# Near positions of keys in two half arrays, and the own block's part added before the write, in a disentangled attention

## The chip, the cores and the metric

The kernel runs on one core of a Trainium2 chip. The metric is the time on the device in microseconds, from the start to the end of one execution. The kernel before took 2058.43 us, the median of three runs (2057.97 to 2059.12).

## The reference, cut to what matters

The program is a chain of four layers on 8 x 512 tokens of 256 channels: an attention with relative positions, a feed-forward layer, a second attention and a layer of routed experts. The change lies in the first attention alone.

```python
q, k, v = split_heads(x @ Wq + bq), split_heads(x @ Wk + bk), split_heads(x @ Wv + bv)   # 16 heads of 16
scores = einsum('bhqd,bhkd->bhqk', q, k) / scale
rel = build_relative_position(S, S, 64, 128)            # buckets of q - k
pos_k = (rel_embeddings @ Wk + bk) by head              # 128 positions
c2p = take_along_axis(einsum('bhqd,hpd->bhqp', q, pos_k), clip(rel + 64, 0, 127))
p2c = take_along_axis(einsum('bhkd,hpd->bhkp', k, pos_k), clip(-rel + 64, 0, 127)) transposed
out = softmax(scores + (c2p + p2c) / scale) @ v
```

The score of a query and a key has three parts: their product; `c2p`, a product of the query with a position that depends on the distance; and `p2c`, a product of the key with such a position. The last one is found by key and has to be turned, so that it lies by query.

## The kernel before, in words

The first attention is cut into 256 steps: 8 batch elements (b), 4 groups of four heads (g), 4 blocks of 128 rows (i), 2 pairs of heads (p). The list `steps` has them in this order, so that a step and the step two later have neighbouring blocks of the same pair of heads. The order of all instructions is written out by hand (`manual_schedule`); each engine takes its own in that order, and waits at semaphores.

For step u, `strips(u)` (it is called in the iteration of step u - 5, `AHEAD`) multiplies 128 queries and 128 keys of two heads with a table of 256 distances. That gives four strips of 128 x 256 (tile `strip`, index 2 j + t: head j; t = 0 by query, t = 1 by key). ScalarE copies them out of PSUM (L371). A row's entry for column c lies at a distance from the diagonal, so the rows have to be shifted against one another. This is done through DRAM: SP writes the strips into a scratch tensor `shift` of rows of 512 (L381), and reads it back with a row step of 511 (L390), which moves each row by one column. In what is read, `winc` has query rows and the key columns of three blocks (two at the first and last block), `winp` has key rows and query columns likewise: 128 x 2 heads x 384 or 256 columns. There are four scratch tensors.

Distances beyond the table have all the value of its last column, `strip[..., W - 1]`. In the own block (key block equal to query block) one triangle lacks it. GpSimd multiplies that value with two triangular masks (`own` from `aside`, L374) and adds the result to the middle block of `winp` and of `winc` (L401), once they are read.

The order on SP's queue is: the write of strip u, then the two reads of strip u - 1 (the list `reads` holds one back). On GpSimd: `own` of u, then the adds of u - 2 (the list `adds` holds two back), then whatever the plan puts into the step.

An iteration n of the main loop does, in the order in which TensorE gets it: products of queries and keys into the score banks `sc` (L421) interleaved with the strips of n + 5 (L364); `near_keys` for each of two heads, which turns the blocks of `winp` and adds them to `sc` (L433: 128 x 128, by a matmul with the identity in transpose mode); VectorE then adds `winc` and finds the row's lowest value (`e`, L447), ScalarE takes the exponential (L450); the turning of the exponentials of the step before (L461, 64 x 64 pieces in alternating halves of the array), which VectorE copies out (L464); and products with the values (L473). `near_keys(n)` reads the windows of steps n - 2, n and n + 2: of n + 2 the first of three blocks, which `own` does not touch. At the last block (i = 3) nothing of n + 2 is needed.

The table `plan` puts further work into certain steps: projections of the next group (L174, two more matmuls of 512 columns twice a step), turning of inputs, values, and the end of a batch element (`finish`), whose `norm` puts six GpSimd operations into each of two successive steps (L521 to L523).

Of the kernel before, what the change touches and what calls it, by code (L numbers as in the profile page):

```python
# [12 lines left out]
F32 = mybir.dt.float32  # L13
# [3 lines left out]
ALU = mybir.AluOpType  # L17
# [4 lines left out]
P = 128  # L22
B, S, H = 8, 512, 256
NT = S // P
# [4 lines left out]
W = 256  # L29
WIN = 3 * P  # L30
# [60 lines left out]
def _l0_attention(nc, tc, a, x, ident, mhalf, carry, prefetch):  # L91
# [6 lines left out]
    with ExitStack() as ctx:  # L98
        pool = lambda name, bufs, **kw: ctx.enter_context(tc.tile_pool(name=name, bufs=bufs, **kw))
        wp = pool("a_w", 1)  # L100
# [44 lines left out]


        winc, cleared = [None] * (2 * NT), list(vs)
        for p in range(2):
            for i, width in ((0, S + 2 * P), (1, S + 3 * P)):
                w = wp.tile([P, 2, width], F32, tag=f"winc{i}{p}", name="winc")  # L150
                cleared.append(w)
                winc[2 * i + p], winc[2 * (NT - 1 - i) + p] = w[:, :, :S], w[:, :, width - S :]
# [37 lines left out]
        with tc.tile_pool(name="a_pos", bufs=1) as pp:  # L190
# [87 lines left out]
            with tc.manual_schedule():  # L278
                nc.vector.memset(pk, 0.0)
                for w in cleared[:3]:  # L280
                    nc.vector.memset(w, 0.0)
                busy(3, zeros)
                measure[0]()
                for n, c in enumerate((P - 1, 0)):
                    f = pp.tile([P, NH, HD], F32, tag=f"end{n}", name=f"end{n}")
                    position_keys(lambda k: relT[:, k, c : c + 1].to_broadcast([P, P]), f)
                    ends.append(f)
                position_keys(lambda k: relT[:, k, :], pk[:, :, :HD])
                some = products()
                next(some)  # L290
                norm[0]()
                next(some)
                measure[1]()
                next(some)
                norm[1]()
                for g in range(NG):
                    for t, dst in ((0, posc), (1, posp)):
                        pe = ps_a.tile([P, S], F32, tag="psa", name="pe")
                        nc.tensor.matmul(
                            pe[:, :W], pk[:, 4 * g : 4 * g + 4, :].rearrange("p h e -> p (h e)"), oh[:, t, :], start=True, stop=True  # L300
                        )
# [24 lines left out]
                for w in cleared[3:]:  # L326
                    nc.vector.memset(w, 0.0)

        sb = pool("a_sb", 2)
# [12 lines left out]
        reads, adds = [], []  # L342
        cns = {b: [] for b in range(B)}
        rest = []
        def project(b, g):
# [10 lines left out]
        def strips(u, between=None):  # L356


            b, g, i, p = steps[u]
            s = sm[b, g]  # L360
            pas = [ps_a.tile([P, S], F32, tag="psa", name="pa") for j in range(2)]
            for t, (src, pos) in enumerate(((s[0], posc), (s[2], posp))):
                for pa, rs in zip(pas, heads(p)):
                    nc.tensor.matmul(  # L364
                        pa[:, t * W : (t + 1) * W], src[rs, i * P : (i + 1) * P], pos[rs, g, :], start=True, stop=True
                    )
                if t == 0 and between is not None:
                    between()
            st = sb.tile([P, 4, W], F32, tag="strip", name="strip", bufs=3)
            for j in range(2):  # L370
                nc.scalar.copy(st[:, 2 * j : 2 * j + 2, :].rearrange("p t w -> p (t w)"), pas[j])  # L371

            own = sb.tile([P, 2, 2, P], F32, tag="own", name="own", bufs=3)
            nc.gpsimd.tensor_tensor(  # L374
                own,
                aside.unsqueeze(2).to_broadcast([P, 2, 2, P]),
                st[:, :, W - 1 : W].rearrange("p (j t) o -> p t j o", t=2).to_broadcast([P, 2, 2, P]),
                ALU.mult,
            )
            d = shift[u % NSHIFT]  # L380
            nc.sync.dma_start(  # L381
                bass.AP(d.tensor, d.offset + P + 1, [[2 * W, P], [2 * W * P, 4], [1, W - 1]]), st[:, :, : W - 1]
            )
# [14 lines left out]

            def add():
                for t, dst in ((1, wk_[:, :, P : 2 * P]), (0, wc[:, :, i * P : (i + 1) * P])):  # L400
                    nc.gpsimd.tensor_tensor(dst, dst, own[:, t], ALU.add)  # L401


            reads.append(read)
            adds.append(add)
# [23 lines left out]
        def near_keys(n, j, sc):  # L429
            i = steps[n][2]  # L430
            lo, hi, c0, c1 = near(i)
            for m in range(lo, hi):
                nc.tensor.matmul(  # L433
                    sc[:, m * P : (m + 1) * P],
                    wins[n + 2 * (m - i)][1][:, j, (i - m + 1) * P : (i - m + 2) * P],
                    ident,
                    start=False,
                    stop=m == hi - 1,
                    is_transpose=True,
                    skip_group_check=True,  # L440
                )

        def weights(n, j, sc):
            b, g, i, p = steps[n]
# [90 lines left out]
        for b in range(B):  # L535
            n = 8 * NG * b
# [18 lines left out]
        with tc.manual_schedule():  # L555
# [9 lines left out]
            for now in range(len(steps) + 3):  # L565
                n = now
                if n < len(steps):
                    b, g, i, p = steps[n]
                    if (i, p) == (0, 0):
                        if g % 2 == 0:  # L570
                            totals[b, g // 2] = sb.tile([P, NT, 8], F32, tag="totals", name="totals", bufs=2)
                    scs, parts = products(n)
                    parts.pop(0)()
                    more = parts.pop() if parts else None
                    if n + AHEAD < len(steps):
                        strips(n + AHEAD, more)
                    else:
                        if more is not None:
                            more()
                        for todo in (reads, adds):  # L580
                            if todo:
                                todo.pop(0)()
                    new = []
# [1087 lines left out]
def _constants():  # L1671
# [12 lines left out]
    for k in range(NK):  # L1684
# [4 lines left out]
    return {  # L1689
        "onehot": onehot,  # L1690
        "tail": tail,
        "later": np.tril(np.ones((P, P), np.float32), -1),
        "before": before,
        "heads": heads,
        "pages": (P * (m[:, None] + P * np.arange(2))).astype(np.float32),
# [74 lines left out]
```

## Time and profile before

| What | Value |
|---|---|
| median of three runs | 2058.43 us |
| profiled execution, its own time | 2059.9 us |
| span from first to last instruction of that execution | 2058.1 us |
| granted TensorE clock, mean of the span | 0.978 |
| first attention, from the first to the last turning of near positions | 44.3 to 1062.3 us |
| TensorE busy in 44 to 1062 us | 993.3 us |
| DMA share and rate in 44 to 1062 us | 0.95, 300 GB/s |
| GpSimd busy in 44 to 1062 us | 732.7 us |
| DMA share in 1062 to 2058 us | 0.43 |

A row of the page's fifth part names line, engine and operation, the output and inputs by the program's names, and the count; then the busy time in us and the mean duration of one in ns; then the idle time of the engine just before such instructions, and what ended most of it. "SPq" is the queue of SP, which issues DMAs; the number behind a kind of DMA is the median time from issue to landing. TensorE's busy time is modelled where matmuls overlap[...].

### The profile page before, as it was taken

How to read it: one execution, taken by the hardware profiler on the slowest of the kernel's cores; microseconds unless marked ns; L12 is line 12 of the kernel's file. 1: busy time of each engine (PE TensorE's matmuls, PEld its weight loads, DVE VectorE, ACT ScalarE, POOL GpSimd, SP SyncE). 2: the span in 40 equal slices, each digit the busy share in tenths (PEclk: the TensorE clock that was granted, in tenths of full speed). 3: DMA queues.
4: the chain of work that ended last, by engine and by line, in shares of the span. 5: the costliest groups of instructions: out<-in, count | busy, mean ns of one | idle time of the engine just before them, and what ended most of it. 6: DMA issues, size and time to landing. Idle time of an engine off the chain costs nothing. (4 is left out here: it accounts for less than half of the span.)

```text
span 2058.1 us, 49708 instructions
## 1 busy us (share of the span) xinstructions
PE 1946.7 (95%) x18056; PEld 1330.7 (65%) x18056; DVE 1393.1 (68%) x3727; ACT 1108.3 (54%) x2370; POOL 1133.2 (55%) x1334
## 2 busy tenths in 40 slices
PE   7999999999999999999989999989898887899997
PEld 4667667676666666666656666645555445588886
DVE  4767777777777777766776555257877786356766
ACT  3777777767776777777742221344343333144443
POOL 4666777867778676776833111014444443455555
PEclk9999999999999999999999999999999998899999
DMA  8999999999999999999964536801111115557888
GB/s 295 332 301 286 306 305 295 312 288 315 297 300 284 296 306 300 296 295 294 293 196 147 155 104 186 21 0 43 43 43 43 43 43 197 199 164 216 269 259 269
DMA packets 387522, 444.46 MB, mean 216 GB/s; under 512 B 43472, under 2 KB 368080, under 8 KB 386768
## 3 DMA queue, kind: packets, MB, share of 16 engines
q1 hardware_dynamic: 372496, 401.94, 64.0%
q0 software_dynamic: 13824, 38.29, 5.1%
q8 instruction: 146, 2.39, 0.5%
q10 hardware_dynamic: 960, 1.05, 0.2%
q14 instruction: 96, 0.79, 0.1%
HBM read 238.99 MB, written 202.19 MB: 214 GB/s over the span
## 5 line engine op out<-in xcount | busy, mean ns | idle before, releaser
L447 DVE CUSTOM_DVE_ANT_0 e<-sc,winc 128x512 f32<-128x512 f32 x512 | 333.4, 689 | 281.0 <-PE sc L433 157.8
L450 ACT ACTIVATE e<-e,low 128x512 f32<-128x512 f32 x512 | 365.6, 715 | 96.0 <-DVE low L447 94.9
L371 ACT COPY strip<-pa 128x512 f32<-128x512 f32 x512 | 275.0, 590 | 128.2 <-POOL winc L401 58.6
L374 POOL TENSOR_TENSOR own<-aside,strip 128x512 f32<-128x512 f32 x256 | 268.5, 1049 | 115.5 <-ACT strip L371 94.3
L464 DVE COPY et<-et_ps 128x512 f32<-128x512 f32 x512 | 328.7, 684 | 0.7 <-PE et_ps L461 0.7
L421 PE MATMUL sc<-sm,sm 32*128 32x256 f32 (+3 forms) x1792 | 309.2, 436 | 0.4
L364 PE MATMUL pa<-pos,sm 32*128 32x256 f32 x2048 | 291.7, 401 | 0.1
L941 POOL DMA_INDIRECT rows<-pay,slot x128 | 141.0, 1101 | 224.2 <-issue 210.9
L401 POOL TENSOR_TENSOR winp<-winp,own 128x256 f32<-128x256 f32 x256 | 186.9, 730 | 107.6 <-DMA winp<-shift 82.1
L421 PEld LDWEIGHTS sc<-sm,sm 32*128 32x128 f32 x1792 | 164.2, 184 | 96.9 <-DVE et L464 34.6
L433 PE MATMUL sc<-ident,winp 128*128 128x128 f32 x1280 | 203.8, 286 | 24.3 <-DMA winp<-shift 23.7
L941 POOL DMA_INDIRECT results<-y,r x160 | 156.0, 975 | 121.0 <-ACT y L1545 78.5
L401 POOL TENSOR_TENSOR winc<-winc,own 128x256 f32<-128x256 f32 x256 | 186.7, 729 | 58.4 <-DMA winc<-shift 48.2
L433 PEld LDWEIGHTS sc<-ident,winp 128*128 128x128 f32 x1280 | 137.1, 141 | 102.7 <-issue 57.9
L461 PE MATMUL et_ps<-ident,e 64*128 64x64 f32 x4096 | 184.1, 230 | 1.1 <-DVE et L464 1.1
L364 PEld LDWEIGHTS pa<-pos,sm 32*128 32x128 f32 x2048 | 175.9, 184 | 10.9 <-ACT strip L371 3.9
L58 POOL TENSOR_TENSOR rstd<-var,mhalf 128x2 f32<-128x2 f32 (+1 forms) x56 | 51.0, 911 | 235.2 <-DVE var L56 212.1
L461 PEld LDWEIGHTS et_ps<-ident,e 64*128 64x128 f32 x4096 | 148.8, 140 | 44.1 <-issue 21.5
L1525 PE MATMUL pge<-store,rT 128*128 x640 | 167.0, 384 | 2.3 <-DMA r<-rows 1.0
L473 PE MATMUL ctx_ps<-et,v 128*32 128x128 f32 x4096 | 167.4, 282 | 0.5 <-DVE et L464 0.5
L174 PE MATMUL pq<-xnT,wqk 128*128 128x512 f32 x256 | 133.3, 645 | 0.0
L738 ACT ACTIVATE hT<-ph,b 128x512 f32<-128x512 f32 x64 | 44.0, 687 | 165.7 <-PE ph L735 165.6
(222 smaller groups left out, 3357.5 us busy)
## 6 DMA issues: line engine op xcount, KB each, us to landing
shift<-strip SPq DMA_DIRECT2D x256, 510.0 KB, 4.5
winp<-shift SPq DMA_DIRECT2D x128, 384.0 KB, 5.4
winc<-shift SPq DMA_DIRECT2D x128, 384.0 KB, 5.5
winp<-shift SPq DMA_DIRECT2D x128, 256.0 KB, 4.1
winc<-shift SPq DMA_DIRECT2D x128, 256.0 KB, 4.4
rows<-empty SPq DMA_DIRECT2D x8, 2640.0 KB, 17.4
r<-rows SPq DMA_DIRECT2D x160, 132.0 KB, 2.5
z<-results SPq DMA_DIRECT2D x32, 512.0 KB, 5.1
```

Source lines behind the costliest of these rows:

```text
L364: nc.tensor.matmul(pa[:, t * W : (t + 1) * W], src[rs, i * P : (i + 1) * P], pos[rs, g, :], start=True, stop=True)
L371: nc.scalar.copy(st[:, 2 * j : 2 * j + 2, :].rearrange("p t w -> p (t w)"), pas[j])
L374: nc.gpsimd.tensor_tensor(own, aside.unsqueeze(2).to_broadcast([P, 2, 2, P]), st[:, :, W - 1 : W].rearrange("p (j t) o -> p t j o", t=2).t ...
L401: nc.gpsimd.tensor_tensor(dst, dst, own[:, t], ALU.add)
L421: nc.tensor.matmul(sc[:, c0:c1], s[side_][rs, cut : cut + P], s[2 + side_][rs, c0:c1], start=c0 == 0, stop=False, skip_group_check=True,)
L433: nc.tensor.matmul(sc[:, m * P : (m + 1) * P], wins[n + 2 * (m - i)][1][:, j, (i - m + 1) * P : (i - m + 2) * P], ident, start=False, stop ...
L447: nc.vector.tensor_tensor_reduce(e, sc, wins[n][0][:, j, :], 1.0, -LOW, ALU.add, ALU.min, low)
L450: nc.scalar.activation(e, e, AF.Exp, bias=low, scale=-1.0, accum_out=totals[b, g // 2][:, i, r : r + 1])
L461: nc.tensor.transpose(bank[:, c : c + 64], e[rs, m * P : (m + 1) * P], ident[rs, rs])
L464: nc.vector.tensor_copy(et[:, f].rearrange("p j m q -> p (j m q)"), bank)
L473: nc.tensor.matmul(ctx_ps[32 * r : 32 * r + 32, i * P : (i + 1) * P], vs[b % 2][:, m, g % 2, g // 2 * 4 + r, :], et[:, :, m, :], start=m = ...
L941: ins = nc.gpsimd.indirect_dma_start(to, bass.IndirectOffsetOnAxis(ap=index, axis=0), source, None, bounds_check=last)
```

## The change

The windows of `winp` get a new layout. Where before 128 rows held a block's keys and two heads side by side, now head j lies in rows 64 j to 64 j + 63, and the second index k is the half of the keys (64 each). For a middle block, the first half of the keys is read with columns 0 to 319 and the second with columns 64 to 383; what the other 64 columns would hold is zero, and is cleared once at the start. So a middle block's read has 320 columns in place of 384; an edge block's has 256 as before. A read of `winp` is now two DMAs, one for each head. The tiles are eight fixed ones in place of a rotating pool of eight.

`near_keys` turns pieces of 64 keys, for head 0 in the upper and head 1 in the lower half of the array, one after the other in turn: twice as many matmuls, each half as wide. It is called once for both heads, ahead of both heads' `e`.

The own block's part is added to the strips before they are written, in place of to the windows after they are read. `own` is the same product with other masks; one GpSimd addition of 128 x 2 x 2 x 128 elements puts it onto a half of each strip. The two additions to the windows, and the list `adds`, are gone. The write now follows the addition. `own` has two buffers in place of three, and the masks are loaded by one DMA.

```diff
+        winp = [wp.tile([P, 2, WIN], F32, tag=f"winp{n}", name=f"winp{n}") for n in range(2 * NT)]
...
-            nc.sync.dma_start(aside[:, 0, :], a["later"])
-            nc.sync.dma_start(aside[:, 1, :], a["earlier"])
+            nc.sync.dma_start(aside, a["aside"])
...
-                for w in cleared[3:]:
+                for w in cleared[3:] + [w.rearrange("p k c -> p (k c)")[:, WIN - 64 : WIN + 64] for w in winp]:
                     nc.vector.memset(w, 0.0)
...
-            own = sb.tile([P, 2, 2, P], F32, tag="own", name="own", bufs=3)
+            own = sb.tile([P, 2, 2, P], F32, tag="own", name="own", bufs=2)
             nc.gpsimd.tensor_tensor(
                 own,
-                aside.unsqueeze(2).to_broadcast([P, 2, 2, P]),
-                st[:, :, W - 1 : W].rearrange("p (j t) o -> p t j o", t=2).to_broadcast([P, 2, 2, P]),
+                aside.unsqueeze(1).to_broadcast([P, 2, 2, P]),
+                st[:, :, W - 1 : W].rearrange("p (j t) o -> p j t o", t=2).to_broadcast([P, 2, 2, P]),
                 ALU.mult,
             )
+            nearer = st.rearrange("p (j t) (h r) -> p j (t h) r", t=2, h=2)[:, :, 0:4:3, :]
+            nc.gpsimd.tensor_tensor(nearer, nearer, own, ALU.add)
             d = shift[u % NSHIFT]
             nc.sync.dma_start(
                 bass.AP(d.tensor, d.offset + P + 1, [[2 * W, P], [2 * W * P, 4], [1, W - 1]]), st[:, :, : W - 1]
             )
             wc = winc[u % (2 * NT)]
-            wk_ = sb.tile([P, 2, WIN], F32, tag="winp", name="winp", bufs=8)
+            wk_ = winp[u % (2 * NT)]

             def read():
                 lo, hi, c0, c1 = near(i)
-                for t, dst in ((1, wk_[:, :, c0:c1]), (0, wc[:, :, lo * P : hi * P])):
+                wide = c1 - c0 == WIN
+                step, c1 = 64 * (2 * W - 1) + 64 * wide, c1 - 64 * wide
+                for j in range(2):
+                    half = wk_[64 * j : 64 * j + 64]
+                    to = half[:, :, c0:c1]
+                    if wide:
+                        to = bass.AP(half.tensor, half.offset, [list(half.ap[0]), [WIN + 64, 2], [1, c1]])
                     nc.sync.dma_start(
-                        dst,
+                        to,
                         bass.AP(
                             d.tensor,
-                            d.offset + t * 2 * W * P + P + c0,
-                            [[2 * W - 1, P], [4 * W * P, 2], [1, c1 - c0]],
+                            d.offset + (4 * j + 2) * W * P + P + c0,
+                            [[2 * W - 1, 64], [step, 2], [1, c1 - c0]],
                         ),
                     )
-
-            def add():
-                for t, dst in ((1, wk_[:, :, P : 2 * P]), (0, wc[:, :, i * P : (i + 1) * P])):
-                    nc.gpsimd.tensor_tensor(dst, dst, own[:, t], ALU.add)
+                lo, hi, c0, c1 = near(i)
+                nc.sync.dma_start(
+                    wc[:, :, lo * P : hi * P],
+                    bass.AP(d.tensor, d.offset + P + c0, [[2 * W - 1, P], [4 * W * P, 2], [1, c1 - c0]]),
+                )
...
-            if len(adds) > 2:
-                adds.pop(0)()
...
+                for k in range(2):
+                    for j, sc in enumerate(scs):
+                        rs, c = slice(64 * j, 64 * j + 64), m * P + 64 * k
+                        nc.tensor.matmul(
+                            sc[:, c : c + 64],
+                            wins[n + 2 * (m - i)][1][rs, k, (i - m + 1) * P : (i - m + 2) * P],
+                            ident[rs, rs],
+                            start=False,
+                            stop=(m, k) == (hi - 1, 1),
...
-                    for j in range(2):
-                        near_keys(n, j, scs[j])
-                        new.append(weights(n, j, scs[j]))
+                    near_keys(n, scs)
+                    new = [weights(n, j, scs[j]) for j in range(2)]
```

More of the change, by code (lines that the diff above doesn't have):

```diff
@@ L341, in _l0_attention @@
         wins, totals = {}, {}
-        reads, adds = [], []
+        reads = []
         cns = {b: [] for b in range(B)}
@@ L384, in strips @@
             wc = winc[u % (2 * NT)]
-            wk_ = sb.tile([P, 2, WIN], F32, tag="winp", name="winp", bufs=8)
+            wk_ = winp[u % (2 * NT)]
             def read():
                 lo, hi, c0, c1 = near(i)
-                for t, dst in ((1, wk_[:, :, c0:c1]), (0, wc[:, :, lo * P : hi * P])):
+                wide = c1 - c0 == WIN
[5 more added lines that the diff above has]
+                        to = bass.AP(half.tensor, half.offset, [list(half.ap[0]), [WIN + 64, 2], [1, c1]])
                     nc.sync.dma_start(
-                        dst,
+                        to,
                         bass.AP(
                             d.tensor,
-                            d.offset + t * 2 * W * P + P + c0,
-                            [[2 * W - 1, P], [4 * W * P, 2], [1, c1 - c0]],
-                        ),
-                    )
-            def add():
-                for t, dst in ((1, wk_[:, :, P : 2 * P]), (0, wc[:, :, i * P : (i + 1) * P])):
-                    nc.gpsimd.tensor_tensor(dst, dst, own[:, t], ALU.add)
+                            d.offset + (4 * j + 2) * W * P + P + c0,
+                            [[2 * W - 1, 64], [step, 2], [1, c1 - c0]],
+                        ),
+                    )
+                lo, hi, c0, c1 = near(i)
[3 more added lines that the diff above has]
+                )
             reads.append(read)
-            adds.append(add)
             if len(reads) > 1:
                 reads.pop(0)()
-            if len(adds) > 2:
-                adds.pop(0)()
             wins[u] = wc, wk_
@@ L427, in products, with near_keys @@
             return scs, parts
-        def near_keys(n, j, sc):
+        def near_keys(n, scs):
             i = steps[n][2]
@@ L432, in near_keys @@
             for m in range(lo, hi):
[L433 to L441, printed above, removed]
+                for k in range(2):
[7 more added lines that the diff above has]
+                            stop=(m, k) == (hi - 1, 1),
+                            is_transpose=True,
+                            skip_group_check=True,
+                        )
         def weights(n, j, sc):
@@ L579, in _l0_attention @@
                             more()
[L580 to L583, printed above, removed]
-                    for j in range(2):
-                        near_keys(n, j, scs[j])
-                        new.append(weights(n, j, scs[j]))
+                        if reads:
+                            reads.pop(0)()
+                    near_keys(n, scs)
+                    new = [weights(n, j, scs[j]) for j in range(2)]
                 if n <= len(steps):
@@ L1691, in _constants @@
         "tail": tail,
-        "later": np.tril(np.ones((P, P), np.float32), -1),
+        "aside": np.stack([(m + m[:, None] >= 127) * (m < 127), m + m[:, None] < 127], 1).astype(np.float32),
         "before": before,
```

## The prediction

> I forecast **2130 us**, slower than the 2058.4 us median. The change shortens TensorE's work, which bounds the kernel, but it moves GpSimd's work in front of the DMA write, and the round trip through DRAM that follows has little slack.
>
> **What bounds the kernel now.** First the page, for the balance and the groups the diff touches; then the stage table; then the DMA view of 200 to 900 us; then the timeline around 500 us.
>
> ```profile
> PE 1946.7 (95%) x18056; PEld 1330.7 (65%) x18056; DVE 1393.1 (68%) x3727; ACT 1108.3 (54%) x2370; POOL 1133.2 (55%) x1334
> ...
> L374 POOL TENSOR_TENSOR own<-aside,strip 128x512 f32<-128x512 f32 x256 | 268.5, 1049 | 115.5 <-ACT strip L371 94.3
> ...
> L401 POOL TENSOR_TENSOR winp<-winp,own 128x256 f32<-128x256 f32 x256 | 186.9, 730 | 107.6 <-DMA winp<-shift 82.1
> ...
> L433 PE MATMUL sc<-ident,winp 128*128 128x128 f32 x1280 | 203.8, 286 | 24.3 <-DMA winp<-shift 23.7
> ```
> ```profile
> 500.00:600.00 100.00, 99.61 (x1380) 69.18 (x1380) 74.10 (x191) 73.75 (x168) 76.17 (x97) 1.00 0.95 298
> ```
> ```profile
> shift<-strip SPq DMA_DIRECT2D x177, 510.0 KB, 4.3
> winp<-shift SPq DMA_DIRECT2D x88, 384.0 KB, 5.4
> ...
> winp<-shift SPq DMA_DIRECT2D x88, 256.0 KB, 4.1
> ```
>
> The reader is to see two near-limits in the first attention. The columns of the stage row are PE, PEld, DVE, ACT, POOL busy, clock, DMA share, GB/s: TensorE is busy 99.6 of 100 us, and the DMA engines 0.95 of the time. And L433, the turning of near positions, is TensorE's one group that waits for DMA: 24 us in all.
>
> By the starts of L433's groups in the timeline, 256 steps run from 44.3 to 1062.3 us: 3.99 us a step, 127.7 us for the 32 steps of one batch element. A bare step takes 3.12 us (4 turns) or 3.23 us (6 turns); one with a projection 4.80, others up to 4.16, repeating in nearly every batch element. That is TensorE's own sum. Exceptions come after runs of bare steps: at the 17th step of a batch element some 2.5 us are lost to the read (615.5 to 617.8 us is one such wait).
>
> **TensorE's part.** Two lines of the timeline show a six-turn step and what the new turns resemble:
>
> ```profile
> 503.15 0.87 PE L433 MATMUL sc<-ident,winp 128*128 128x128 f32 x6
> ...
> 503.96 0.71 PE L461 MATMUL et_ps<-ident,e 64*128 64x64 f32 x16
> ```
>
> From L433's start to L461's start 6 full turns take 0.81 us, 135 ns each. L461 has exactly the new shape (64 rows, 64 columns, alternating halves of the array, each half its own bank), and its 16 take 0.71 us, 44 ns each with the ending. The change makes 12 such of 6, or 8 of 4. Middle blocks: 0.87 - 12 x 0.044 = 0.34 us less; edge blocks: 4 x 0.135 - 8 x 0.040 = 0.22 less; mean 0.28, times 256: **72 us** if nothing else bound. [...] The trace's 44 ns for the same form decides; I take 0.28.
>
> **DMA bytes.** A step moves 510 KB out and on average 2 x 320 KB in. In half the steps 64 KB of `winp` go: 32 of 1150 KB, 2.8%. The engines are busy 0.95 x 3.99 = 3.79 us a step, so 3.68 afterwards, 118 us for 32 steps. This is a floor under every case, near TensorE's new sum: 127.7 less 9 of turns less some 3.5 of stalls = 115.
>
> **What moves.** Before, SP writes a strip as soon as ScalarE's copies end. `own` runs on GpSimd beside the write, and the two adds come after the reads; near blocks of a neighbour need no add, so turning waits for the read alone. After, `own` and the new add on the strip both stand before the write. The new add has 512 elements, two full inputs. No such row is in this stage; bounds are `own` (1.05 us, one input a broadcast) and two L401 adds (1.46). The nearest is the add of `bproj`, the same size with two inputs read once:
>
> ```profile
> L1120 POOL TENSOR_TENSOR x<-x,bproj 128x512 f32<-128x512 f32 x16 | 19.9, 1273 | 0.1
> ```
>
> So the write starts 0.1 + 1.01 (start to start in the timeline) + 1.27 = **2.4 us later** (2.2 to 2.6). Behind the waiting write on SP stand all three reads of the strip before. GpSimd's busy sum even falls (2.51 to 2.32 us a step), which earns nothing.
>
> **The round trip.** The turns of step n need the read of strip n+2, whose products run in step n-3. So from the turns of n-4 to those of n the least time is: rest of a bare step to the strip's products, 2.9 (3.23 - 0.34, or 3.12 - 0.22); ScalarE's copies 1.2 (products end 503.22, copies 504.40); GpSimd 2.4; the write's landing 4.3; SP's read 0.1; the read's landing. For the last, 384 KB take 5.4 and 256 KB 4.1, so 320 KB some 4.75, and the mean over middle and edge is 4.4. The waiting turn comes 0.2 into its group, the semaphore costs 0.1: -0.1. Sum **15.2 us a hop**, plus what step n-4 carries besides (projection and so on). By the step lengths, the extras at steps 0, 4, ... 28 are 1.57, 0.93, 1.57, 0, 1.57, 0.46, 1.57, 0.93: 8.6. Eight hops: 121.6 + 8.6 = 130.2 us against 127.7.
>
> The same sum before: 3.2 + 1.2 + 0 + 4.3 + 0.1 + 4.75 - 0.1 = 13.45; eight are 107.6 + 8.6 = 116.2, which leaves 1.4 us slack a hop. It was covered; 2.4 us more isn't, and TensorE's faster turns only reach the wait sooner. Cost: 2.5 x 8 = **+20 us**.
>
> [...] The trace prices only the second issue: 0.36 to 0.45 us on SP. The write issued just before keeps the engines filled meanwhile, so I take 0; if that cover is gone 0.4 us a hop, 26 us.
>
> **GpSimd's bursts.** Once for each of seven batch elements, two successive steps put six adds each (L521 to L523) on GpSimd:
>
> ```profile
> 501.20 0.36 SPq L381 DMA_DIRECT2D shift<-strip  x1
> ...
> 505.19 0.73 POOL L522 TENSOR_TENSOR xn<-xn,ln_bias 128x256 f32<-128x256 f32 x1
> ...
> 508.31 0.73 POOL L523 TENSOR_TENSOR x<-x,xn 128x256 f32<-128x256 f32 x1
> 509.00 1.05 POOL L374 TENSOR_TENSOR own<-aside,strip 128x512 f32<-128x512 f32 x1
> ```
>
> This `own` belongs to the strip written at 501.20: it is 7.8 us late, and nobody suffers, as the write has long gone. Matched in order, that lag is 5.9 us in the mean of seven. Afterwards the write waits for it. 7 x 5.9 = **+41 us**; ends 0 (if GpSimd caught up before) and 55.
>
> **Clock.** After the wait of 2.3 us at 617.8, four projections took 3.64 us instead of some 1.6, and the granted clock of 609 to 626 was 0.80. Longer burst waits would do that too; I take 1.5 us of each, **+10** (0 to 25).
>
> **At nothing or little.** Eight clears of 128x128 on VectorE at the start, beside the first round trip (longer by 2.4): **+3** together. One constant load for two: 0. Both heads turned before the first `e`: VectorE starts about 0.1 us later on the first, earlier on the second; 0, since it idles a quarter of the stage. `own` with two buffers: its reader follows on the same engine, 0. A strip's buffer comes free 2.4 us later, with three in use and 12 us between: 0.
>
> **Sum.** 20 + 41 + 10 + 3 = +74 on the profiled 2059.9 us (span 2058.1): 2134; the median of the runs lies 1.5 lower, so about 2132, rounded to 2130.
>
> **Rivals.**
> 1. The round trip shrinks (20%). With fewer bytes and writes and reads spaced by GpSimd, the engines' backlog falls; landings 0.6 and 0.5 us shorter give 14.1 a hop, 121.4 for 32 steps, above the 118 floor; bursts half hidden, +3. Then 124.4 against 127.7: -26 us, +3 at the start: **2035**. At full bursts it decides from 74 / 64 = 1.2 us less a hop. For it: 256 KB reads already land in 4.1. Against: reads always follow a fresh write of 510 KB. TensorE's and DMA's floors together allow at best 1980.
> 2. The round trip grows (17%): reads queue right behind the write, as the 5.4 us row suggests, landings 0.9 longer per hop: 7.2 x 8 = 58 more, **2190**.
> 3. No visible difference (3%), gain and loss cancelling: 2058. About 0.2% is what a measurement of this kernel can tell from none.
> 4. The turns don't pack[...]: TensorE is then no faster[...], inside my forecast's case (60%, 2065 to 2180).
>
> **Range.** 2045 to 2190: half a microsecond on both landings moves a hop enough for 64 us, the add's bounds 13, the bursts' -41 to +14. Left out are the better half of rival 1 and the worse of rival 2. Faster 0.20, same 0.03, slower 0.77.
>
> **What would show it.** Right: new turns 40 to 50 ns each; a write following a GpSimd add, not ScalarE's copy, by 2.2 to 2.6 us; TensorE's busy share in the stage falling to some 90%, its turns waiting for `winp` reads for 100 us or more in all; DMA share 0.85 to 0.92; two long gaps near the L521 to L523 bursts of each batch element. Wrong: the stage still at 99% with steps of 2.9 us, or DMA at 1.0, or landings under 4 us.

## The result and the profile after

The changed kernel takes 2251.3 us (median; 2236.8 to 2254.1) against 2058.8 us for the kernel before on the same chip: ratio **1.0915, 95% interval 1.0887 to 1.0944**, 193 us slower. The profiled execution took 2254.06 us, with a span of 2252.1 us and a mean granted clock of 0.931 (before 0.978). In the experiments below, each ratio is taken against the kernel before in runs beside it, where its median was 2065.4 to 2070.0 us.

First the stage table of the changed kernel; its columns are again the stretch, its length, busy time of PE, PEld, DVE, ACT and POOL, the clock, the DMA share and GB/s:

```profile
500.00:600.00 100.00, 86.24 (x1202) 57.47 (x1203) 58.98 (x146) 59.70 (x134) 60.98 (x61) 0.88 0.81 235
```

Nothing is at its limit any more: TensorE is busy 86 of 100 us, the DMA engines 0.81 of the time, GpSimd 0.61. When no engine is full and the time still grows, a chain through several of them sets it. The page shows who waits:

```profile
PE 1997.3 (89%) x19336; PEld 1351.9 (60%) x19336; DVE 1391.9 (62%) x3735; ACT 1110.0 (49%) x2370; POOL 1098.3 (49%) x1078
...
L374 POOL TENSOR_TENSOR own<-aside,strip 128x512 f32<-128x512 f32 x256 | 268.4, 1048 | 383.3 <-ACT strip L371 346.8
...
L381 POOL TENSOR_TENSOR strip<-strip,own 128x512 f32<-128x512 f32 x256 | 325.4, 1271 | 20.1
...
L445 PE MATMUL sc<-ident,winp 64*128 64x64 f32 x2560 | 185.6, 247 | 168.0 <-DMA winp<-shift 166.7
```

TensorE stood still for 168 us ahead of its turns (24.3 before), and the read of `winp` ended 166.7 of that. GpSimd idles 347 us until ScalarE's copies are there, and does its new addition, 1271 ns, in front of the write. The waits of SP's queue in 200 to 900 us (total, times, longest), first one line of the kernel before, then the changed kernel:

```profile
SPq L381 <- ACT strip L371: 264.5, 172, 5.4
```
```profile
SPq L383 <- POOL strip L381: 167.7, 113, 4.7
SPq L383 <- ACT strip L371: 62.0, 30, 4.1
SPq L400 <- DMA shift<-strip: 57.0, 55, 2.1
```

Before, the write (L381) waited for ScalarE's copies; now (L383) it mostly waits for the addition on GpSimd. The reads (L400) of the strip before stand behind it in the same queue.

One hop of the chain, in the timeline of the changed kernel (start, duration, engine, line, operation, and in brackets the idle time before):

```profile
497.21 1.07 ACT L371 COPY strip<-pa 128x512 f32<-128x512 f32 x2 [0.36 <-issue]
...
498.36 1.05 POOL L374 TENSOR_TENSOR own<-aside,strip 128x512 f32<-128x512 f32 x1 [0.67 <-ACT strip L371]
...
499.49 1.26 POOL L381 TENSOR_TENSOR strip<-strip,own 128x512 f32<-128x512 f32 x1
499.65 0.27 PE L445 MATMUL sc<-ident,winp 64*128 64x64 f32 x1 [2.28 <-DMA winp<-shift]
...
500.98 0.42 SPq L383 DMA_DIRECT2D shift<-strip  x1
502.64 3.78 PE L175 MATMUL pq<-xnT,wqk 128*128 128x512 f32 x4
...
509.17 1.98 PE L175 MATMUL pq<-xnT,wqk 128*128 128x512 f32 x4
```

The copies begin at 497.21 and end at 498.28; the strip's write starts only at 500.98. Meanwhile a turn waits 2.28 us for an earlier strip's read. The last two lines show a second cost: four projections take 3.78 us shortly after that wait, and 1.98 us in the next step, which has no wait. The granted clock was 0.50 in 502.6 to 506.5 us and 0.95 in 506.5 to 511.2.

**Where the time went.** By the starts of the turns in the timeline, the first attention now runs from 44.0 to 1258.4 us, 196 us more than before (44.3 to 1062.3). What comes after it takes 994 us in place of 996. So all the loss is in the first attention: 4.76 us a step in place of 3.99.

To see which part of the round trip carries it, the starts of its parts were taken for 61 hops, each from the turn of step n-4 that needs a read to that of step n, and averaged (us):

| From to | before | after | as forecast for after |
|---|---|---|---|
| turn of n-4 to end of the strip's products | 4.36 | 4.94 | 2.9 + 1.08 extras |
| to end of the copies | 1.08 | 1.07 | 1.2 |
| to the write's issue (GpSimd) | 0.03 | 2.56 | 2.4 |
| write's issue to read's issue | 5.05 | 5.11 | 4.4 |
| read's issue to the turn | 5.38 | 5.27 | 4.3 |
| hop | 15.91 | 18.95 | 16.28 |

The hop grew by 3.04 us, 64 hops give 195 us: the whole loss. It is GpSimd's 2.53 and 0.58 on TensorE's part, which the half clock lengthens. The two DMA legs stayed where they were: nothing in them gave way to take up the delay.

For the first of the two, the queue shows why. Two lines of SP in the changed kernel:

```profile
494.72 0.37 SPq L383 DMA_DIRECT2D shift<-strip  x1
495.19 1.43 SPq L400 DMA_DIRECT2D winp<-shift  x2
```

The read leaves right behind the write of the *next* strip. It does so (within 0.6 us) in 52 of the 61 hops, and in 43 before. So this leg is mostly the distance between two successive writes (4.56 us in the mean, 4.32 before), and not the time in which one write lands. In the change GpSimd holds up both writes alike, and a late write does not shorten the leg behind it.

### The profile page after: what moved, and what is told of

Same layout as the page of the kernel before. It is cut to its first block, busy times and chain, and to the rows that moved or that the text cites. A ratio compares the mean times of both kernels' runs of the same rounds, so it can differ in the third digit from the quotient of the medians.

```text
span 2252.1 us, 51933 instructions
## 1 busy us (share of the span) xinstructions
PE 1997.3 (89%) x19336; PEld 1351.9 (60%) x19336; DVE 1391.9 (62%) x3735; ACT 1110.0 (49%) x2370; POOL 1098.3 (49%) x1078
## 3 DMA queue, kind: packets, MB, share of 16 engines
q8 instruction: 156, 2.56, 0.5%
q10 hardware_dynamic: 960, 1.05, 0.2%
## 4 chain that ended last, share of the span: by engine, by line
PE 41%; POOL 17%; DVE 13%; issue 13%; DMA 12%; ACT 2%; SPq 2%; POOLq 0%; DVEq 0%; ACTq 0%
DMA winp<-shift 8%; POOL strip L381 7%; POOL own L374 6%; PE pge L1534 6%; PE po L752 5%; PE pq L175 3%; PE poe L1552 3%; PE sc L429 3%; DMA shift<-strip 3%; PE ph L744 2%; PE ctx_ps L485 2%; PE et_ps L473 2%; PE sc L445 2%; DVE prod L867 2%; PE pq L1017 2%
## 5 line engine op out<-in xcount | busy, mean ns | idle before, releaser
L429 PE MATMUL sc<-sm,sm 32*128 32x256 f32 (+3 forms) x1792 | 353.2, 457 | 0.6 <-DVE low L459 0.3
L381 POOL TENSOR_TENSOR strip<-strip,own 128x512 f32<-128x512 f32 x256 | 325.4, 1271 | 20.1
L445 PE MATMUL sc<-ident,winp 64*128 64x64 f32 x2560 | 185.6, 247 | 168.0 <-DMA winp<-shift 166.7
L364 PE MATMUL pa<-pos,sm 32*128 32x256 f32 x2048 | 307.4, 418 | 0.4 <-ACT strip L371 0.2
L445 PEld LDWEIGHTS sc<-ident,winp 64*128 64x128 f32 x2560 | 125.3, 144 | 268.7 <-DMA winp<-shift 191.0
L429 PEld LDWEIGHTS sc<-sm,sm 32*128 32x128 f32 x1792 | 181.3, 194 | 126.7 <-DVE et L476 45.3
L364 PEld LDWEIGHTS pa<-pos,sm 32*128 32x128 f32 x2048 | 184.5, 193 | 11.5 <-ACT strip L371 4.3
L485 PE MATMUL ctx_ps<-et,v 128*32 128x128 f32 x4096 | 183.4, 302 | 0.0
L473 PEld LDWEIGHTS et_ps<-ident,e 64*128 64x128 f32 x4096 | 170.0, 152 | 1.8 <-ACT e L462 1.4
L175 PE MATMUL pq<-xnT,wqk 128*128 128x512 f32 x256 | 162.3, 767 | 0.7 <-PE pv L157 0.7
L186 ACT ACTIVATE sm<-pq,bias 128x512 f32<-128x512 f32 x128 | 81.1, 684 | 97.2 <-PE pq L175 93.9
```

The lines of the kernel that those rows point to most:

```text
L364: nc.tensor.matmul(pa[:, t * W : (t + 1) * W], src[rs, i * P : (i + 1) * P], pos[rs, g, :], start=True, stop=True)
L381: nc.gpsimd.tensor_tensor(nearer, nearer, own, ALU.add)
L429: nc.tensor.matmul(sc[:, c0:c1], s[side_][rs, cut : cut + P], s[2 + side_][rs, c0:c1], start=c0 == 0, stop=False, skip_group_check=True,)
L445: nc.tensor.matmul(sc[:, c : c + 64], wins[n + 2 * (m - i)][1][rs, k, (i - m + 1) * P : (i - m + 2) * P], ident[rs, rs], start=False, stop ...
L473: nc.tensor.transpose(bank[:, c : c + 64], e[rs, m * P : (m + 1) * P], ident[rs, rs])
```

## The experiments

The theory after the result was: the addition in front of the write lengthens the round trip, and this alone makes the loss; TensorE's gain is wasted. Rivals: the reads in halves of 64 rows; the half clock after each wait; the queueing behind SP's write.

### Which part of the change

**Without the addition** (from the changed kernel). The dependence of the write on GpSimd goes, its work stays:

```diff
-            nc.gpsimd.tensor_tensor(nearer, nearer, own, ALU.add)
+            nc.gpsimd.tensor_tensor(own, own, own, ALU.add)
```

> The changed kernel with the addition taken off the strips (GpSimd adds own to itself instead, so its work stays the same): the write follows ScalarE's copies again. It leaves out the own block's part for far distances. Theory 'round trip' (the GpSimd pair in front of the write is what TensorE waits for): the waits for winp fall from 167 us to under 40, the clock of the first attention returns to 0.98, and the turns in halves show their gain: 1980 to 2020 us. Rival 'halves' (reading 64 rows in two DMAs and turning in halves is slow by itself): still above 2150 us.

Measured: 1.0195 (1.0146 to 1.0244), 2109.6 against 2069.2 us. GpSimd's part of the hop falls from 2.56 to 0.30 us and most of the loss goes. But the kernel is still 40 us slower than before, though TensorE has less to do. The time lies between the two expectations: the addition is not the whole cause.

**The addition alone** (from the kernel before: reads and turns as they were, the masks and the addition of the change):

```diff
+            nearer = st.rearrange("p (j t) (h r) -> p j (t h) r", t=2, h=2)[:, :, 0:4:3, :]
+            nc.gpsimd.tensor_tensor(nearer, nearer, own, ALU.add)
...
-            adds.append(add)
...
-            if len(adds) > 2:
-                adds.pop(0)()
```

> The kernel before with one part of the change: own is added to the strips ahead of the write, reads and turns stay as they were (128 rows, 384 columns, whole array). 'Round trip': the same 2.4 us in front of the write, TensorE's own sum 67 us longer than after the change: waits of 100 to 150 us and a lower clock, 2180 to 2270 us. 'Halves': within 1% of before, 2040 to 2080 us.

Measured: 1.0917 (1.0869 to 1.0966), 2259.8 us. Its group of turns on the page, and its 200 to 900 us:

```profile
L427 PE MATMUL sc<-ident,winp 128*128 128x128 f32 x1280 | 223.9, 296 | 155.9 <-DMA winp<-shift 155.5
```
```profile
200.00:900.00 700.00, 615.83 (x7967) 411.43 (x7969) 434.51 (x1081) 428.85 (x967) 411.21 (x395) 0.93 0.81 250
```

The addition alone makes the full loss and the changed kernel's picture: 155.5 us of waits for `winp`, DMA share 0.81. Its hop is 19.06 us, the change's 18.95. Under this chain, the faster turns and the fewer bytes of the change are worth nothing.

**The reads in halves alone** (from the kernel before: `winp` keeps its layout, but is read as rows 0 to 63 and 64 to 127):

```diff
-                for t, dst in ((1, wk_[:, :, c0:c1]), (0, wc[:, :, lo * P : hi * P])):
+                for f in range(2):
                     nc.sync.dma_start(
-                        dst,
+                        wk_[64 * f : 64 * f + 64, :, c0:c1],
...
```

> The kernel before with one part of the change: winp is read by two DMAs of 64 rows each, the same bytes to the same places, everything else as before. In e1 the packets of these reads took 75.6 ns (1280 bytes) and 92.6 (1536), where before 1536 bytes took 78.0. Theory 'two DMAs slow the engines': the same lengthening of the mean, DMA at its limit, 2090 to 2130 us. If the packets were slowed by TensorE's quicker pace or by the new columns: 2055 to 2068 us.

Measured: 1.0316 (1.0269 to 1.0362), 2139.4 against 2068.2 us, a little more than the first theory expected. TensorE's turns wait 71.9 us for `winp` in place of 23.7. The prediction had priced this at nothing, and at 26 us if its cover was gone. Against it stands a control with **two reads of all 128 rows**, one for each head:

```diff
-                for t, dst in ((1, wk_[:, :, c0:c1]), (0, wc[:, :, lo * P : hi * P])):
+                for j in range(2):
                     nc.sync.dma_start(
-                        dst,
+                        wk_[:, j, c0:c1],
...
```

> The kernel before with winp read by two DMAs as in e5, but cut by head and not by rows: each goes to all 128 rows with half of the bytes. 'Rows'[...]: mean packets at 78 ns again and 2055 to 2075 us. 'Number' (one DMA more a step is what costs): like e5, 2120 us or more.

Measured: 1.004 (1.002 to 1.0061), 2079.1 against 2070.0 us. One more DMA in the queue costs 9 us, a little more than expected; that it reaches only 64 rows costs 62 more. The DMA views for 200 to 900 us show it in the bytes (packets, MB, share of the 16 engines), first of before, then of the 64-row reads, then of the control:

```profile
q1 hardware_dynamic: 189747, 208.04, 94.8%
```
```profile
q1 hardware_dynamic: 180260, 194.53, 94.3%
```
```profile
q1 hardware_dynamic: 189762, 205.36, 94.3%
```

At the same share of busy engines 219 MB per unit of share went through before (208.04 / 0.948), 218 in the control, and 206 with 64-row reads: 6% less. In the records of the packets, those of 1536 bytes take 78.0 ns in the mean before, 79.9 in the control and 90.2 here, with the median at 65 in all: a tail of slow packets. Why reads into 64 rows make for slower packets, no run shows; at 94% busy engines, with other traffic beside, the price was 6% of throughput.

### The clock and the queue

**Filled waits** (from the changed kernel): at the steps where the longest waits come, three or four matmuls on data that is there, into a bank that nobody reads, keep TensorE going:

```diff
+                    if n % 8 == 0 or n % 32 == 20:
+                        busy(3 if n % 32 == 8 else 4, posc[:, 0:2].rearrange("p g w -> p (g w)"))
                     near_keys(n, scs)
```

> The changed kernel with three or four extra matmuls of 512 columns (0.64 us each at full clock), with results that nobody reads, just ahead of the turns of each group's first step and of one more step a batch element, where its trace waits 2 to 4.6 us. 'Clock' (half of the loss is the time at half clock after a wait, 259 us of it against 34 before): granted clock of the first attention 0.97 or more and 2130 to 2180 us. If the waits alone are the loss: 2240 to 2260 us, or longer where the extra matmuls don't fit.

Measured: 1.0791 (1.0737 to 1.0844), 2229.0 us, 22 us less than the change. This lies between the two expectations. TensorE's own account would put much on the clock: its turns wait 143 us longer than before (166.7 against 23.7), 232 us more at half clock cost at most half of that, 116 (four projections took 3.78 us at a clock of 0.50 and 1.98 at 0.95), and the shorter turns give back 67 (worked out below): together 192 of the 196 us. But here the time that the first attention spends at half clock falls from 259 us to 92 us (27 before, by the same count), and the gain is 1.1%. In the hop, TensorE's part falls from 4.94 to 3.90 us, but the read's leg grows from 5.27 to 5.78 and GpSimd's from 2.56 to 2.78. This speaks for a half clock that mostly fills time which the round trip takes anyway. The test isn't clean, since the extra matmuls take time of their own (0.59 us each in the median).

**The write from GpSimd's own queue** (from the changed kernel), so that SP's reads no longer stand behind a write that waits:

```diff
-            nc.sync.dma_start(
+            nc.gpsimd.dma_start(
                 bass.AP(d.tensor, d.offset + P + 1, [[2 * W, P], [2 * W * P, 4], [1, W - 1]]), st[:, :, : W - 1]
             )
```

> The changed kernel with the write of a strip issued from GpSimd's queue right after the addition, in place of SP's: a read no longer stands behind the next strip's write on SP. The trace of the change has 1.84 us in the mean, and 4 to 5 us at the steps that then wait, from the write's landing to the issue of the read's second half. 'Behind the write' (that queueing is a large part of the wait): 2120 to 2200 us. If the chain through the same strip sets the wait: 2240 us or more, with GpSimd's issue cost on top.

Measured: 1.0983 (1.0938 to 1.1029), 2274.3 us: no better. TensorE waits 173.9 us for `winp`, against 166.7. GpSimd's busy time in 200 to 900 us rises from 412.0 to 523.6 us, and its instructions there from 399 to 535: about one more a strip, 0.82 us each, which fits the issue of the write. The queueing itself did go: in the 30 hops where the landing is on record, the read is issued 0.05 us after its own strip's write has landed (1.33 us after it in the change, over 47 hops). But from issue to landing that write takes 4.92 us there in place of 3.82, and GpSimd's part of the hop grows from 2.57 to 3.52. One cost was replaced by others, so the run can't say that queueing costs nothing; it doesn't support it as the main cause.

### Giving the round trip more time

If the chain sets the time, strips made earlier should bring it back. The lead is one constant (the distance `AHEAD` from making a strip to using it). **Lead 6**, for the changed kernel and for the one before:

```diff
-AHEAD = 5
+AHEAD = 6
...
```

(The rest keeps a loop at the start from loading an input that isn't there.)

> The changed kernel with strips computed six steps ahead of their use in place of five. 'Round trip': each read gets one more step, about 3.6 us, near to the whole of the longest common wait; what is left is the DMA engines' limit that e1 showed: 2080 to 2130 us. If it stays above 2200 us, the round trip isn't what TensorE waits for.

> The kernel before with strips six steps ahead in place of five. Its waits for winp are 24 us and TensorE's own sum fills the rest: 2030 to 2055 us if the waits go, and no more than that, since what is left is TensorE's sum.

Measured: the change 1.0591 (1.0555 to 1.0627), 2196.8 us; the kernel before 1.0846 (1.0814 to 1.0879), 2244.1 us. The waits for `winp` are gone (6.9 us and 2.8 us), but TensorE itself got slower, and both miss their expectations. Two views of the kernel before with lead 6, the windows and the timeline; then the same work with lead 5:

```profile
200.00:900.00 700.00, 700.00 (x8085) 489.80 (x8084) 437.71 (x1093) 440.03 (x981) 435.75 (x553) 1.00 0.82 252
```
```profile
511.49 0.51 PE L421 MATMUL sc<-sm,sm 32*128 32x128 f32 x3
511.82 0.38 PE L364 MATMUL pa<-pos,sm 32*128 32x256 f32 x1
511.84 0.27 PE L421 MATMUL sc<-sm,sm 32*128 32x128 f32 x1
511.95 0.59 PE L364 MATMUL pa<-pos,sm 32*128 32x256 f32 x3
512.25 0.94 PE L421 MATMUL sc<-sm,sm 32*128 32x384 f32 x4
512.89 0.72 PE L364 MATMUL pa<-pos,sm 32*128 32x256 f32 x4
```
```profile
501.95 0.51 PE L421 MATMUL sc<-sm,sm 32*128 32x128 f32 x2
502.09 0.48 PE L364 MATMUL pa<-pos,sm 32*128 32x256 f32 x2
502.16 0.73 PE L421 MATMUL sc<-sm,sm 32*128 32x128 f32 x4
```

TensorE is busy 700.00 of 700 us, with the clock at 1.00, and is slower: a bare step takes 3.97 us in place of 3.12. Products (L421) and strips (L364) start at 511.49 and reach the turns at 513.55, 2.06 us; with lead 5 the same work took 1.20 us (501.95 to the turns at 503.15). With an odd lead the two interleaved streams work on opposite pairs of heads, so on different rows of the array, and took the 1.20 us; with an even lead they share the rows, and took the 2.06 (4 and 3.9 us for the change's bare steps with lead 6, too, and 3.12 again in the kernel before with lead 7). So of the leads 5, 6 and 7 only the odd ones keep the short step. A busy share of 100% did not show this loss; only the length of the same work did.

**Lead 7**: before, addition alone, and change. The projections come a step earlier and each read a step later, so that data and buffers fit (in the kernel before also one buffer more for `own` and one less for `et`):

```diff
-AHEAD = 5
+AHEAD = 7
...
-            if len(reads) > 1:
+            if len(reads) > 2:
...
-                slot((n + 8 * g - 8, n + 8 * g - 7), project(b, g))
+                slot((max(n + 8 * g - 9, 0), n + 8 * g - 8), project(b, g))
...
-            slot((n + 24, n + 25), project(b + 1, 0))
+            slot((n + 23, n + 24), project(b + 1, 0))
...
```

> The kernel before with strips seven steps ahead, reads held back two, adds three, projections one step earlier. e7 (six ahead) had no waits left but put strips and products into the same row groups, 0.85 us more in each step; seven keeps them apart. 2025 to 2050 us: the waits of the first attention (24 us in all) go, TensorE's own sum stays.

> e2 (own added to the strips ahead of the write, reads and turns as before) with strips seven steps ahead, reads held back two strips, and the projections one step earlier, so that strips and products stay in different row groups of the array. 'Round trip': the 2.4 us are covered by one or two steps more, 2030 to 2075 us where e2 took 2260. If the addition costs in another way (GpSimd's bursts, the scratch write itself): above 2150 us.

> The changed kernel with strips seven steps ahead, reads held back two, projections one step earlier. 'Round trip' plus 'slow half-row reads': the waits for the round trip go, and what stays is the DMA engines' limit, at e1's level or a little under: 2060 to 2110 us, DMA share 0.95 or more. If only the round trip costs: 1990 to 2020 us.

Measured: the kernel before 1.004 (1.0016 to 1.0063), 2079.5 us; the addition alone 1.0139 (1.0111 to 1.0167), 2098.5; the change 1.0057 (1.0039 to 1.0075), 2080.8. The kernel before doesn't gain from the lead, having few waits to lose (24.3 us down to 1.7), and misses its expectation; so the edits that came with the lead don't make it faster by themselves. The other two lose nearly all their loss: from 1.0917 to 1.0139 (less than expected), and from 1.0915 to 1.0057. The round trip's length against its lead was the cause of nearly all of it. With lead 7 the change and the kernel before are equal.

What was left stands at one step of each batch element. The addition alone with lead 7, in the timeline:

```profile
514.48 1.28 POOL L380 TENSOR_TENSOR strip<-strip,own 128x512 f32<-128x512 f32 x1
...
515.78 0.36 SPq L382 DMA_DIRECT2D shift<-strip  x1
...
519.64 0.72 POOL L517 TENSOR_TENSOR x<-x,xn 128x256 f32<-128x256 f32 x1
520.32 1.04 POOL L373 TENSOR_TENSOR own<-aside,strip 128x512 f32<-128x512 f32 x1
521.44 1.28 POOL L380 TENSOR_TENSOR strip<-strip,own 128x512 f32<-128x512 f32 x1
...
522.75 0.36 SPq L382 DMA_DIRECT2D shift<-strip  x1
```

Between two writes, 515.78 and 522.75, lie 7 us, because the six normalizing operations come first on GpSimd. By the starts of the turns, step 21 of a batch element then takes 7.6 us (median) where the kernel before with lead 7 takes 3.7, and no other step is more than 0.2 us longer than there; with the change it is 8.0 in place of 3.3. So the last edit **spreads the burst**, one tile of three operations a step, on the change with lead 7. It also moves products of the output away from the steps just before a projection:

```diff
-            def norm(first, bank, pool):
-                for t in (first, first + 1):
...
+            def norm(t, bank, pool):
...
-            slot((n + 36, n + 37, n + 38, n + 39, n + 40, n + 41, n + 48, n + 49), [partial(f, misc, sb) for f in done])
+            slot((n + 36, n + 37, n + 38, n + 41, n + 42, n + 43, n + 47, n + 48, n + 55, n + 56), [partial(f, misc, sb) for f in done])
```

> e11 with the end of a batch element spread: its six-operation bursts on GpSimd cut into four of three, at steps that carry a projection, and its products of the output kept off the steps just before a projection. In e11 the step after the second burst took 8.0 us where TensorE's own work is 3.3, once in each of seven batch elements. 'Bursts' (the write waits behind them): 33 us less, and 14 more from the step before the first projection: 2030 to 2050 us. 'DMA limit' (share 0.96 in e11, 3.83 us of the engines' time a step): little less than 2060 us, whatever GpSimd does.

Measured: **0.9938 (0.9917 to 0.9959)**, 2055.0 against 2065.4 us: 0.6% less than the kernel before, and 1.2% less than with lead 7 alone, nearer to the second of the two expectations. Its turns and its 200 to 900 us:

```profile
L445 PE MATMUL sc<-ident,winp 64*128 64x64 f32 x2560 | 158.0, 238 | 30.5 <-DMA winp<-shift 28.9
```
```profile
200.00:900.00 700.00, 676.61 (x10731) 462.06 (x10732) 540.25 (x1327) 529.66 (x1192) 506.21 (x489) 1.00 0.99 298
```

TensorE has slack (676.6 of 700; 690.9 before), and now the DMA engines are the fullest, at 0.99. By this row they bound it, which would explain why 67 us less work on TensorE bring only 10 us here, and would make it the place where the 64-row reads' lost throughput is paid.

Not tried: half turns with `winp` read over all 128 rows. There both halves of the array would write into one bank, since a head lies over all rows, and no run shows what that costs. So what the half turns would bring without the 64-row reads stays open. Nor was the spread burst tried on the kernel before, so the parts of the last version's gain aren't told apart.

## Why the prediction was wrong

The sign and the mechanism (GpSimd's work in front of the write, paid by TensorE's waits) were right, the size was not: +74 us forecast, +193 measured, outside the range and above the second rival's 2190. The step that failed is the third below.

- **TensorE's part**, near in its sum, in part by luck. Where none waits, twelve new turns take 0.58 us and eight 0.46 us with the ending, and 0.43 and 0.30 us to the next group's start (0.81 and 0.59 before): 35 to 38 ns each by starts, where 40 to 50 were named. The two halves' turns start in pairs: in the row below the two of a pair lie 3 to 4 ns apart, and the next pair follows 57 to 61 ns later (108 after the first pair). The sum of the shortest typical step lengths falls from 123.8 to 115.4 us for 32 steps, 67 us in all (72 forecast). But the steps share it otherwise: one with a projection gains 0.34 us (4.80 to 4.46), a bare one only 0.08 (3.23 to 3.15, 3.12 to 3.03), where 0.34 and 0.22 were put. A bare step of the changed kernel:

```profile
512.16 0.58 PE L445 MATMUL sc<-ident,winp 64*128 64x64 f32 x12
...
513.49 0.69 DVE L459 CUSTOM_DVE_ANT_0 e<-sc,winc 128x512 f32<-128x512 f32 x1
513.75 0.29 PEld L429 LDWEIGHTS sc<-sm,sm 32*128 32x128 f32 x2 [0.20 <-DVE low L459]
...
514.24 0.18 PEld L429 LDWEIGHTS sc<-sm,sm 32*128 32x128 f32 x1 [0.20 <-DVE low L459]
```

The next step's products (L429) wait for VectorE to finish with the score banks, once for each head. In an edge block (step 111 of 256, counted from 0) TensorE comes to these products 0.33 us earlier than before (1.47 in place of 1.80 us after the start of the turns), but VectorE is done with the second bank only 0.08 us earlier (1.92 in place of 2.00). So "0, since it idles a quarter of the stage" missed that VectorE's time to the end of its work counts here, not its share.

- **The write later by 2.4**, right: 2.50 us in the median, with 1.05 and 1.27 us of work on GpSimd.
- **"The round trip … leaves 1.4 us slack a hop. It was covered"**: this step failed. The sum put the two DMA legs of the kernel before at 9.05 us (8.7 after), and they measure 10.4 in both kernels. The 1.4 us between are the whole slack: it stood in the sum alone. The sum made the first leg from a write's landing. But the read mostly leaves behind the next strip's write, which waited for ScalarE's copies before and waits for GpSimd now; the prediction names this order and doesn't price it. So the loop had nothing to give: of GpSimd's 2.53 us the two legs took up 0.05. The term of +20 should have been some 2.53 x 64 = 162 us, which includes the bursts where they hit these hops.
- **Halved reads at 0**, wrong. Alone they cost 71 us (62 beyond a plain second DMA). The prediction priced the second issue alone; the greater cost was in the rows each read reaches. In the hop the second read also leaves 0.67 us after the first (median). Within the full change it is hidden: the addition alone is as slow as the change. The floor of 118 us for 32 steps fell with it: without the addition the DMA engines are at 0.95 and a step still takes 4.19 us, 134 for 32.
- **Bursts +41**, of the right kind. Step 20 of each batch element takes 8.7 us where it needs 3.3, about 5 a burst; with lead 7, where they stand alone, the excess is 3.9 to 4.7, so 27 to 33 us for seven. Only this one step stands out behind the bursts, where two long gaps were named. And the greater stalls are at steps 0, 8, 16 and 24 (10.0, 7.2, 11.0 and 9.8 us, own need 4.46): the last two steps of a group need no later strip and run ahead, and the next one pays for the hops before.
- **Clock +10**, wrong in size: 232 us more at half clock. But filling the waits brought back only 22 us, so it doesn't seem to be what made up the gap. (The "some 1.6" there is what projections add to a step; a row of four without a wait takes 1.98 us.)
- **Rival 2**, a longer trip, named the missing part at half its size: it put 0.9 us more on the DMA legs of a hop, and they measure 1.7 more (10.4 against 8.7). They were that long before, too: not the change made them longer, as the rival had it, but the sum had them too short. Rival 1, a shrinking backlog, came in part and earned nothing: the share fell to 0.81 and reads of `winc` land in 4.8 us in place of 5.5 (384 KB, median), but the legs didn't move.
- **What would show it**: waits of 100 us or more (166.7), a write 2.2 to 2.6 us behind (2.50), TensorE near 90% (608 of 700, 87%) came; the DMA share fell below the 0.85 named, the sign that the loss would be larger.

## What to carry to other kernels

A step put in front of a write, whose read-back something waits for, is to be priced on the whole loop and not on its engine, even if that engine gets less to do; the slack of the loop is to be measured between the starts of its parts (issue to issue, issue to use) and not added up from median landings. A loop that is too long can be started earlier in place of shortened, but look first at which rows of the array the interleaved streams then share (with lead 6 a bare step took 3.97 us in place of 3.12). With DMA engines that are nearly full, as here, a read over half the rows can cost more than one more DMA over all of them (62 us beside 9).

## What was not expected of the hardware

- Two interleaved streams of matmuls with 32 rows took 1.20 us where their rows differ (lead 5) and 2.06 us where they share them (lead 6): a bare step takes 3.12 and 3.97 us, with TensorE busy all the time in both.
- Reads into 64 rows cost 6% of the throughput of the whole queue at 94% busy engines, by a tail: mean packet 90.2 ns in place of 78.0, median the same 65.
- Waits of 1.5 to 4.0 us (medians) at five of 32 steps, and shorter ones elsewhere, were enough for 259 us at half clock in 1214, in stretches of some 3.4 us and multiples of it; the page's mean of 0.931 doesn't show how much of it lies on the path.
- Shorter turns shortened a bare step by 0.08 us only, though TensorE counts as busy all through it: a wait for VectorE stood behind them that the busy share doesn't show.
